# Layers 1 to 3 of a four-layer convolution stack: statistics and quantisation in other steps of a round, layer 1 two chunks behind layer 2, zeros written at the edges only

## The chip, the cores and the metric

The kernel runs on one core of one Trainium2 chip. The metric is the device time of one execution in microseconds (us). Shown are the times of three runs and their median; the profile is of one more execution, whose own time stands beside its span in the table below.

## What is computed

The input x is 32 images of 8 channels of 256 x 256, f32. Four layers follow each other, each of the form x + conv(group norm(x)), with 4 groups of 2 channels:

```python
def _gn(v, G=4, eps=1e-5):           # mean and variance over a group of one image
    ...
x = x + _L0_conv_ref(_gn(x), ...)    # a coupled map lattice of 15 steps, a small network, a gate
x = x + _L1_conv_ref(_gn(x), w, b)   # 3x3, 8 -> 8, on values quantised to +-127
x = x + _L2_conv_ref(_gn(x), w, b)   # 3x3, 8 -> 8, f32
x = x + _L3_conv_ref(_gn(x), w)      # 5x5 mean of each channel
```

Layer 1 quantises with one scale for the whole batch, `sx = 127 / max|gn(x)|`, so it cannot begin before layer 0 has ended for all 32 images. The values of layer 1 are whole numbers up to 127 and are held in bf16; everything else is f32.

## The kernel before

Layer 0 (lines 168 to 676) takes most of the time and isn't touched. Its last step for each image leaves the mean and 1/deviation in `stat1`, the largest normalised value in `peak1`, and the image in DRAM (`x1_d`).

**Layout of layers 1 to 3 (from line 679).** One image is one tile of 128 partitions x 4096: a partition is a pair of (one of 16 rows of a block, one of 8 channels), and the free axis holds 16 blocks of 256 columns. A 3x3 convolution of two blocks (512 columns, one PSUM tile `psv`, one chunk) is `conv3`, line 721: three matmuls over all 128 partitions, one for each column offset (L725), and one for the rows that lie in the neighbouring blocks (L729). The latter reads a small tile of neighbours (`qb` for layer 1, `xb2` for layer 2) of 72 partitions, of which 48 carry data: `beside`, line 138, fills them by two DMAs of 24 partitions from the image's own tile (`qh`, `xh`), issued from the SP queue. An f32 matmul is two records in the profile, a bf16 matmul one. There are 8 chunks (NCH) in an image.

**Tiles and zeros.** `qh`, `qb`, `xh`, `xb2`, `xr` and `xr2` are made once and are reused by all images; lines 718 and 719 set them wholly to zero, on POOL (GpSimd), before the loop. Later only the inner part is rewritten, so that the borders stay zero. The loads of `x1` (L736) are issued from the POOL queue too, behind those memsets. The quantisation scale (`top`, line 150, and lines 694 to 708) is made on DVE in the same stretch.

**A round.** The loop at line 863 runs 35 rounds. In round b, layer 1 works on image b, layer 2 on image b-1, the normalisation of layer 3 on image b-2 and layer 3 itself on image b-3. The order on each engine is the program's order, written out by hand (`manual_schedule`)[...].

The first part of a round is `layer3`, a generator of 8 steps (two for each of 4 groups; PE: L811 and L824, DVE: the addition L831). `among` (line 844) runs one step and then the tasks listed for that step. The tasks in before are

- steps 0 to 3: one piece each of the statistics of layer 2's output (`parts3`) and of layer 1's output (`parts`). `stats_parts`, line 95, has after its first piece, L101, these four: a matmul that averages means (L104) and four small DVE operations (L105 to L108); a second matmul (L111) and one DVE operation (L112); a square root on ACT (L115); five small DVE operations (L117 to L121)
- steps 0 to 3: `quantize1`, a quarter of the image each (DVE L741, L703, L704, then ACT L705), called q0 to q3 below
- step 3: `normal2` (DVE L760, 128 x 4096) ahead of q3, and its two DMAs for `xb2`
- step 4: the two DMAs for `qb`
- step 5: `by_group` (line 127), the statistics of layer 2's output by channel group: two DVE operations (L131), a matmul (L133) that waits for them, and a copy (L135)

The second part of a round runs layers 2 and 1 by turns: one chunk of layer 2 (PE L725, L729; DVE L770 adds, L771 gathers statistics), then one chunk of layer 1 (PE the same lines with bf16; ACT L754, DVE L755 and L756), eight times. In its first four turns `normal3` (DVE L792) prepares layer 3's input `xr`, and after the fourth `beside3` issues two DMAs. At the end of the round `begin` adds up both statistics (L101), the 16 stores of layer 2's output go out from the POOL queue (L776), and the load of `y` for layer 3 (L785) and of the next `x1` stand behind them.

Of the kernel before, what the change touches and what calls it, by code (L numbers as in the profile page):

```python
# [9 lines left out]
F32 = mybir.dt.float32  # L10
BF16 = mybir.dt.bfloat16
# [9 lines left out]
HB = 16  # L21
RB = H // HB
HP, WP = H + 2, W + 2
# [37 lines left out]
def window(ap, offset, dims):  # L61

    return bass.AP(ap.tensor, ap.offset + offset, [list(d) for d in dims])
# [3 lines left out]
def kernel(  # L67
# [3 lines left out]
    nc = tc.nc  # L71
    B = x.shape[0]
# [54 lines left out]
    def by_group(psum, st):  # L127

        sel = small.tile([P, 4, 2], F32, name="sel")
        for j in range(2):  # L130
            nc.vector.tensor_scalar(sel[:, :, j], gsel_sb, st[:, j : j + 1], None, ALU.mult)  # L131
        ps = psum.tile([P, 512], F32, name="ps")
        nc.tensor.matmul(ps[:, 0:8], ones, sel.rearrange("p a b -> p (a b)"), start=True, stop=True)  # L133
        got = small.tile([P, 4, 2], F32, name="got")
        nc.vector.tensor_copy(got.rearrange("p a b -> p (a b)"), ps[:, 0:8])  # L135
        return got

    def beside(queue, t, src, q):


        row, long = HB * WP, (HB - 1) * WP - 2
        for i, (p, to, at) in enumerate(((P - C, 1, 0), (0, 0, 1))):
            queue.dma_start(
                t[q + 24 * i : q + 24 * i + 24, :, :].rearrange("p k w -> p (k w)")[
                    :, to * WP : to * WP + long
                ],
                window(src, p * row + at * WP, [[row, C], [1, 3], [1, long]]),
            )
# [19 lines left out]
    with ExitStack() as es:  # L168
        wt = es.enter_context(tc.tile_pool(name="wt0", bufs=1))
# [5 lines left out]
        psum = es.enter_context(tc.tile_pool(name="ps_a", bufs=3, space=PSUM))  # L175
# [503 lines left out]
    with ExitStack() as es:  # L679
        wt = es.enter_context(tc.tile_pool(name="wt1", bufs=1))  # L680
        two = es.enter_context(tc.tile_pool(name="two", bufs=2))
        psum = es.enter_context(tc.tile_pool(name="ps_b", bufs=3, space=PSUM))
# [19 lines left out]
        def quantize(dst, t, s):  # L702
            nc.vector.tensor_scalar(t, t, s, MAX_Q, ALU.mult, ALU.min)  # L703
            nc.vector.tensor_scalar(t, t, -MAX_Q, ROUND, ALU.max, ALU.add)  # L704
            nc.scalar.activation(dst, t, AF.Copy, bias=-ROUND)  # L705
# [3 lines left out]


        qh = wt.tile([P, HB, WP], BF16, name="qh")
        qb = wt.tile([72, HB, WP], BF16, name="qb")
        xh = wt.tile([P, HB, WP], F32, name="xh")
        xb2 = wt.tile([72, HB, WP], F32, name="xb2")

        xr = wt.tile([P, 2, C, W + 4], F32, name="xr")
        xr2 = wt.tile([72, C, W + 4], F32, name="xr2")
        for t in (qh, qb, xh, xb2, xr, xr2):
            nc.gpsimd.memset(t, 0.0)

        def conv3(src, near, w, i):
            ps = ps_v.tile([P, 512], F32, name="psv")
            o = ps.rearrange("p (k w) -> p k w", w=W)
            for dx in range(3):
                nc.tensor.matmul(  # L725
                    o, w[:, dx, :], src[:, 2 * i : 2 * i + 2, dx : dx + W],
                    start=dx == 0, stop=False,
                )
            nc.tensor.matmul(  # L729
                o, w[0:72, 3, :], near[:, 2 * i : 2 * i + 2, 0:W], start=False, stop=True  # L730
            )
            return ps

        def load1(b):
            x1 = two.tile([P, NPX], F32, name="x1")
            nc.gpsimd.dma_start(x1, x1_d[b])  # L736
            return x1

        def quantize1(b, x1, k):
            t = two.tile([P, 1024], F32, name="tq")  # L740
            nc.vector.tensor_scalar(  # L741
                t, x1[:, bass.ts(k, 1024)], stat1[:, b, 0:1], stat1[:, b, 1:2],
                ALU.subtract, ALU.mult,
            )
            quantize(
                qh[:, 4 * k : 4 * k + 4, 1 : 1 + W],
                t.rearrange("p (r w) -> p r w", w=W), sc[:, 0:1],
            )
# [10 lines left out]
        def normal2(x2, st):  # L759
            nc.vector.tensor_scalar(  # L760
                xh[:, :, 1 : 1 + W], x2.rearrange("p (k w) -> p k w", w=W),
                st[:, 0:1], st[:, 1:2], ALU.subtract, ALU.mult,
            )
            beside(nc.sync, xb2, xh, 0)

        def layer2(b, x2, bn):
            for i in range(NCH):
                ps = conv3(xh, xb2, w2_sb, i)
                c = x2[:, bass.ts(i, 512)]
                nc.vector.scalar_tensor_tensor(c, ps, b2_sb, c, ALU.add, ALU.add)  # L770
                nc.vector.bn_stats(bn[:, i, :], c)  # L771
                yield
            x3 = x3_d[b % 2]
            for r in range(RB):
                m = r % 4 * 4 + r // 4
                nc.gpsimd.dma_start(  # L776
                    window(x3, r * W, [[H * W, C], [RB * W, HB], [1, W]]),
                    x2[C * m : C * m + C, :].rearrange("p (k w) -> p k w", w=W),
                )
# [10 lines left out]
        def normal3(y, gs, g):  # L790
            for k in range(2):
                nc.vector.tensor_scalar(  # L792
                    xr[:, k, 2 * g : 2 * g + 2, 2 : 2 + W], y[:, k, 2 * g : 2 * g + 2, :],
                    gs[:, g, 0:1], gs[:, g, 1:2], ALU.subtract, ALU.mult,
                )
# [46 lines left out]
        x1s, x2s, ys, gss, sums = {}, {}, {}, {}, {}  # L842

        def among(work, tasks):
            for i in range(8):
                next(work, None)
                for task in tasks.get(i, ()):
                    task()
            for _ in work:
                pass  # L850

        def step(parts):
            return lambda: next(parts, None)

        def begin(bn):
            st = small.tile([P, 2], F32, name="st")
            parts = stats_parts(psum, bn, st, gavr_sb, "ps")
            next(parts)
            return st, parts

        with tc.manual_schedule():
            x1s[0] = load1(0)
            for b in range(B + 3):
                if b + 1 < B:
                    x1s[b + 1] = load1(b + 1)
                tasks = {i: [] for i in range(8)}
                if 2 <= b <= B + 1:
                    st3, parts3 = sums.pop(2)
                    for i in range(4):
                        tasks[i].append(step(parts3))  # L870

                    def groups():
                        gss[b - 2] = by_group(psum, st3)

                    tasks[5].append(groups)
                if 1 <= b <= B:
                    st, parts = sums.pop(1)
                    for i in range(4):
                        tasks[i].append(step(parts))
                    tasks[3].append(lambda: normal2(x2s[b - 1], st))  # L880
                if b < B:
                    for k in range(4):
                        tasks[k].append(lambda k=k: quantize1(b, x1s[b], k))
                    tasks[4].append(lambda: beside(nc.sync, qb, qh, 0))
                among(layer3(b - 3, ys.pop(b - 3)) if b >= 3 else iter(()), tasks)
                tasks = {}
                if 2 <= b <= B + 1:
                    for g in range(4):
                        tasks[g] = [lambda g=g: normal3(ys[b - 2], gss[b - 2], g)]
                    tasks[3].append(beside3)  # L890
                bns = [small.tile([P, NCH, 6], F32, name="bn") for _ in range(2)]
                if b < B:
                    x2s[b] = two.tile([P, NPX], F32, name="x2")
                ones_ = layer1(b, x1s[b], x2s[b], bns[0]) if b < B else iter(())

                def both():
                    for _ in layer2(b - 1, x2s[b - 1], bns[1]) if 1 <= b <= B else range(8):
                        next(ones_, None)
                        yield

                among(both(), tasks)
                if 1 <= b <= B:
                    sums[2] = begin(bns[1])
                    ys[b - 1] = load3(b - 1)
                if b < B:
                    sums[1] = begin(bns[0])
# [136 lines left out]
```

## Time and profile before

| | us |
|---|---|
| three runs | 16305.33, 16277.27, 16303.53 |
| median | 16303.53 |
| the profiled execution, its time | 16318.33 |
| its span | 16316.6 |
| mean granted clock of PE | 0.961 |

Busy time over the span, of the page: PE 15452.2 (95%), DVE 11705.9 (72%), ACT 5726.7 (35%), POOL 5598.2 (34%). The page's slices of the span are 407.9 us each; the 34th, where PE falls to seven tenths and POOL to three, is the passage from layer 0 to the rest. The last operation of layer 0 on DVE (L581) is at 13611.19, and layers 1 to 3 take from there to the end, some 2,700 us.

| line, operation | count | mean ns |
|---|---|---|
| L725 PE, layer 2, 128x512 f32 | 1536 | 629 |
| L725 PE, layer 1, 128x512 bf16 | 768 | 384 |
| L729 PE, layer 2, 72 rows, f32 | 512 | 600 |
| L729 PE, layer 1, 72 rows, bf16 | 256 | 399 |
| L811 PE, layer 3 | 2560 | 600 |
| L824 PE, layer 3, 72 rows to 32 columns | 512 | 608 |
| L760 DVE normal2 | 32 | 2415 |
| L741, L703, L704 DVE, a quarter of the quantisation | 128 each | 834, 791, 719 |

How to read it: a matmul's duration in the records is longer than the distance to the next one, since matmuls overlap; PE's pace is read from start to start. A wait is shown as idle time before an instruction with the instruction or DMA that ended it. PE's clock is halved in stretches, and the page gives the granted share in tenths.

### The profile page before, as it was taken

How to read it: one execution, taken by the hardware profiler on the slowest of the kernel's cores; microseconds unless marked ns; L12 is line 12 of the kernel's file. 1: busy time of each engine (PE TensorE's matmuls, PEld its weight loads, DVE VectorE, ACT ScalarE, POOL GpSimd, SP SyncE). 2: the span in 40 equal slices, each digit the busy share in tenths (PEclk: the TensorE clock that was granted, in tenths of full speed). 3: DMA queues.
4: the chain of work that ended last, by engine and by line, in shares of the span. 5: the costliest groups of instructions: out<-in, count | busy, mean ns of one | idle time of the engine just before them, and what ended most of it. 6: DMA issues, size and time to landing. Idle time of an engine off the chain costs nothing.

```text
span 16316.6 us, 141125 instructions
## 1 busy us (share of the span) xinstructions
PE 15452.2 (95%) x42888; PEld 6215.7 (38%) x42888; DVE 11705.9 (72%) x14652; ACT 5726.7 (35%) x8862; POOL 5598.2 (34%) x9491
## 2 busy tenths in 40 slices
PE   6999999999999999999999999999999997999999
PEld 2333333333333333333333333333333332333333
DVE  7777777777777777777777777777777764555554
ACT  2433444443434434443434444343444442111110
POOL 1333333333333333333333333333333342111111
PEclk7999999999999999999999999999999998999999
DMA  4766666666666666666666666666666664555554
GB/s 104 148 146 144 150 147 144 147 150 146 149 144 148 150 147 147 144 147 145 147 142 149 148 144 147 141 148 146 147 149 147 146 134 98 119 119 119 119 118 105
DMA packets 1057742, 2276.12 MB, mean 139 GB/s; under 512 B 419740, under 2 KB 623508, under 8 KB 1050724
## 3 DMA queue, kind: packets, MB, share of 16 engines
q0 software_dynamic: 704512, 1492.80, 40.6%
q1 hardware_dynamic: 352484, 774.29, 23.4%
q8 instruction: 356, 5.83, 0.2%
q14 instruction: 390, 3.19, 0.1%
HBM read 1078.04 MB, written 471.38 MB: 95 GB/s over the span
## 4 chain that ended last, share of the span: by engine, by line
PE 74%; DVE 13%; DMA 7%; ACT 3%; issue 2%; SPq 1%; POOL 0%; DVEq 0%; ACTq 0%; POOLq 0%
PE ph L633 17%; PE psc L391 14%; PE psc L393 13%; PE pg L531 9%; DVE acc L338 7%; PE psv L725 5%; PE pn L610 5%; PE psv L811 4%; DMA qb<-qh 3%; DMA rings<-state 2%; PE psv L729 2%; PE pq L548 1%; PE pg L543 1%; PE pg L539 1%; DVE psc L402 1%
## 5 line engine op out<-in xcount | busy, mean ns | idle before, releaser
L338 DVE SCALAR_TENSOR_TENSOR acc<-strip,taps_sb,acc 128x1024 f32<-128x1024 f32 x3840 | 4930.4, 1284 | 124.8 <-DMA strip<-strip 4.7
L505 POOL DMA_DIRECT2D im<-xn_d x6144 | 3458.3, 566 | 3250.0 <-PE ph L633 1434.7
L633 PE MATMUL ph<-im,wp_sb 72*128 72x512 f32 x8192 | 4091.7, 615 | 308.8 <-ACT hh L638 251.3
L638 ACT ACTIVATE hh<-ph,bp_sb 128x512 f32<-128x512 f32 x4096 | 2755.8, 690 | 4441.9 <-PE ph L633 4385.7
L402 DVE SCALAR_TENSOR_TENSOR psc<-psc,flat 128x512 f32<-128x512 f32 x2880 | 1921.4, 696 | 2813.0 <-PE psc L393 2797.2
L391 PE MATMUL psc<-state,patch_sb 128*128 128x512 f32 x5760 | 2812.0, 626 | 74.1 <-ACT state L419 63.3
L393 PE MATMUL psc<-rings,ring_sb 80*128 80x512 f32 x5760 | 2713.5, 607 | 129.8 <-DMA rings<-state 129.8
L633 PEld LDWEIGHTS ph<-im,wp_sb 72*128 72x128 f32 x8192 | 1489.5, 193 | 2425.4 <-issue 1587.8
L419 ACT ACTIVATE state<-psc,minus 128x512 f32<-128x512 f32 x2688 | 1690.2, 690 | 1818.8 <-DVE psc L402 1713.1
L391 PEld LDWEIGHTS psc<-state,patch_sb 128*128 128x128 f32 x5760 | 1114.5, 199 | 1696.2 <-issue 1375.7
L393 PEld LDWEIGHTS psc<-rings,ring_sb 80*128 80x128 f32 x5760 | 1114.7, 194 | 1576.8 <-issue 1545.7
L569 POOL DMA_DIRECT2D x_d<-xc x256 | 146.9, 574 | 3493.1 <-DVE xc L564 3416.6
L811 PE MATMUL psv<-xr,w_sb 128*128 128x512 f32 x2560 | 1162.9, 600 | 1.3 <-DVE xr L792 1.3
L610 PE MATMUL pn<-hh,wu_sb 128*32 128x512 f32 x8192 | 1133.9, 609 | 3.3 <-ACT hh L638 3.3
L776 POOL DMA_DIRECT2D x_d<-x x512 | 321.0, 643 | 1941.0 <-DVE x L770 1696.3
L725 PE MATMUL psv<-xh,w_sb 128*128 128x512 f32 x1536 | 753.0, 629 | 9.6 <-issue 9.6
L531 PE MATMUL pg<-xq,wg_sb 128*128 128x512 f32 x1536 | 749.3, 626 | 0.0
L754 ACT ACTIVATE x<-psv,b_sb,sc 128x512 f32<-128x512 f32 x256 | 199.3, 779 | 1466.2 <-PE psv L729 1465.8
L531 PE MATMUL pg<-cq,wg_sb 128*128 128x512 f32 x1536 | 713.7, 601 | 0.0
L811 PEld LDWEIGHTS psv<-xr,w_sb 128*128 128x128 f32 x2560 | 466.1, 189 | 610.8 <-issue 606.0
L338 DVE SCALAR_TENSOR_TENSOR acc<-strip,taps_sb,d 128x1024 f32<-128x1024 f32 x480 | 613.2, 1277 | 0.0
L831 DVE TENSOR_TENSOR y<-psv,y 128x512 f32<-128x512 f32 x256 | 177.1, 692 | 593.7 <-PE psv L811 593.7
(163 smaller groups left out, 12188.9 us busy)
## 6 DMA issues: line engine op xcount, KB each, us to landing
im<-xn_d POOLq DMA_DIRECT2D x6144, 96.6 KB, 6.6
rings<-state SPq DMA_DIRECT2D x1920, 159.5 KB
rings<-state SPq DMA_DIRECT2D x1920, 106.3 KB
strip<-strip SPq DMA_DIRECT2D x960, 126.0 KB
xn_d<-xb POOLq DMA_DIRECT2D x128, 516.0 KB, 7.7
nr_d<-xb POOLq DMA_DIRECT2D x128, 516.0 KB, 7.2
xq<-nr_d POOLq DMA_DIRECT2D x128, 516.0 KB, 5.1
cq<-cr_d POOLq DMA_DIRECT2D x128, 516.0 KB, 7.9
```

What stands on the lines that cost most here:

```text
L338: nc.vector.scalar_tensor_tensor(acc, strip[:, dy : dy + RQ, dx : dx + W], taps_sb[:, 3 * dy + dx : 3 * dy + dx + 1], d2 if dy == 1 and dx ...
L391: nc.tensor.matmul(pss[-1], patch_sb[:, c, :], inner(c), start=True, stop=False)
L393: nc.tensor.matmul(pss[c % HALF], ring_sb[:, c, :], rings[half][:, c % HALF, 0 : TX * SY].rearrange("p (x y) -> p x y", y=SY)[:, :, 0:TY], ...
L402: nc.vector.scalar_tensor_tensor(ps, ps, FLOOR, dr[:, c], ALU.max, ALU.add)
L419: nc.scalar.activation(inner(c), pss[c % HALF], AF.Square, bias=minus)
L505: nc.gpsimd.dma_start(im[24 * dy : 24 * dy + 24, k, 0:run], window(xn_d[b % 3], at, [[HP * WP, C], [1, 3], [1, run]]),)
L531: nc.tensor.matmul(o, wg1_sb[:, s, dx, :], src[:, :, dx : dx + W], start=s == dx == 0, stop=False,)
L610: nc.tensor.matmul(pn[32 * q : 32 * q + 32, :], wu_sb[:, i, :], hh, start=i == 0, stop=i == 3,)
L633: nc.tensor.matmul(ph.rearrange("p (k w) -> p k w", w=W), wp_sb, im[:, :, j * WP : j * WP + W], start=True, stop=True,)
L638: nc.scalar.activation(hh, ph, AF.Relu, bias=bp_sb)
L725: nc.tensor.matmul(o, w[:, dx, :], src[:, 2 * i : 2 * i + 2, dx : dx + W], start=dx == 0, stop=False,)
L811: nc.tensor.matmul(pss[k].rearrange("p (c w) -> p c w", w=W), w3_sb[:, dx, :], xr[:, k, mine, dx : dx + W], start=dx == 0, stop=stop,)
```

## The change

Layer 0 isn't touched (its lines move by one). In layers 1 to 3:

- **Zeros.** Only borders are set to zero, by twelve small memsets on DVE; `xr2` alone keeps its memset on POOL. `qb` and `xb2` shrink to the 48 partitions that carry data, and the edge matmul (L740 in the new file) reads 48 rows.
- **Statistics of layer 1's output**: the four pieces stand in steps 0, 0, 1, 1 (they stood in 0 to 3), and `normal2` with its DMAs in step 1 (it stood in step 3).
- **Statistics of layer 2's output**: in steps 1 to 4 (they stood in 0 to 3). `by_group` is split: its DVE part in step 4, its matmul and copy in step 6 (both stood in step 5).
- **Quantisation**: q0 in step 0, q1 and q2 in step 2, q3 in step 3 (they stood in 0, 1, 2, 3), and the DMAs for `qb` in step 3 (they stood in step 4).
- **Layer 1 runs two chunks behind layer 2**: turns 0 and 1 have layer 2 alone, turns 2 to 7 both, and the last two chunks of layer 1 follow one after the other.

```diff
     def by_group(psum, st):
         ...
+        yield None
         ps = psum.tile([P, 512], F32, name="ps")
         ...
-        return got
+        yield got
...
-        qb = wt.tile([72, HB, WP], BF16, name="qb")
+        qb = wt.tile([48, HB, WP], BF16, name="qb")
         xh = wt.tile([P, HB, WP], F32, name="xh")
-        xb2 = wt.tile([72, HB, WP], F32, name="xb2")
+        xb2 = wt.tile([48, HB, WP], F32, name="xb2")
...
-        for t in (qh, qb, xh, xb2, xr, xr2):
-            nc.gpsimd.memset(t, 0.0)
+        for t in (qh, xh):
+            for w in (0, WP - 1):
+                nc.vector.memset(t[:, :, w : w + 1], 0.0)
+        for t in (qb, xb2):
+            for k in (0, HB - 1):
+                nc.vector.memset(t[:, k, :], 0.0)
+        for k in range(2):
+            for w in (0, W + 2):
+                nc.vector.memset(xr[:, k, :, w : w + 2], 0.0)
+        nc.gpsimd.memset(xr2, 0.0)
...
-                o, w[0:72, 3, :], near[:, 2 * i : 2 * i + 2, 0:W], start=False, stop=True
+                o, w[0:48, 3, :], near[:, 2 * i : 2 * i + 2, 0:W], start=False, stop=True
...
+                if 1 <= b <= B:
+                    st, parts = sums.pop(1)
+                    for i in range(4):
+                        tasks[i // 2].append(step(parts))
+                    tasks[1].append(lambda: normal2(x2s[b - 1], st))
                 if 2 <= b <= B + 1:
                     st3, parts3 = sums.pop(2)
                     for i in range(4):
-                        tasks[i].append(step(parts3))
+                        tasks[i + 1].append(step(parts3))
+                    parts4 = by_group(psum, st3)
+                    tasks[4].append(step(parts4))
 
                     def groups():
-                        gss[b - 2] = by_group(psum, st3)
-
-                    tasks[5].append(groups)
-                if 1 <= b <= B:
-                    st, parts = sums.pop(1)
-                    for i in range(4):
-                        tasks[i].append(step(parts))
-                    tasks[3].append(lambda: normal2(x2s[b - 1], st))
+                        gss[b - 2] = next(parts4)
+
+                    tasks[6].append(groups)
                 if b < B:
                     for k in range(4):
-                        tasks[k].append(lambda k=k: quantize1(b, x1s[b], k))
-                    tasks[4].append(lambda: beside(nc.sync, qb, qh, 0))
+                        tasks[(0, 2, 2, 3)[k]].append(lambda k=k: quantize1(b, x1s[b], k))
+                    tasks[3].append(lambda: beside(nc.sync, qb, qh, 0))
...
                 def both():
-                    for _ in layer2(b - 1, x2s[b - 1], bns[1]) if 1 <= b <= B else range(8):
-                        next(ones_, None)
+                    twos = layer2(b - 1, x2s[b - 1], bns[1]) if 1 <= b <= B else iter(range(8))
+                    for i, _ in enumerate(twos):
+                        if i > 1:
+                            next(ones_, None)
                         yield
+                    for _ in ones_:
+                        pass
```

## The prediction

> **What bounds the kernel now.** The changed lines run only after the last stage-0 matmul, so I first read the slices of the page (PE at nine tenths nearly everywhere, a dip at the 34th) and then, for 13,590 us to the end, PE's timeline, PE's waits and DVE's timeline. In the steady rounds PE is never more than a few microseconds from its next matmul, so a round costs PE's own work plus its waits. PE's waits from 13,900 to 16,150 us (total, times, longest):
>
> ```profile
> PE psv L729 <- DMA qb<-qh: 104.9, 28, 5.6
> PE ps L133 <- DVE sel L131: 28.4, 27, 1.1
> ```
>
> Two waits per round are all there is. PE's timeline of one round shows both and what follows (start, length, instruction, idle before it):
>
> ```profile
> 14291.24 8.85 PE L811 MATMUL psv<-xr,w_sb 128*128 128x512 f32 x20
> 14300.02 1.05 PE L824 MATMUL psv<-xr,w3h_sb 72*32 72x512 f32 x4
> 14301.01 1.98 PE L811 MATMUL psv<-xr,w_sb 128*128 128x512 f32 x4
> 14304.04 0.39 PE L133 MATMUL ps<-sel,ones 128*128 128x8 f32 x2 [1.05 <-DVE sel L131]
> ...
> 14399.22 0.81 PE L725 MATMUL psv<-qh,w_bf 128*128 128x512 bf16 x3
> 14403.53 0.39 PE L729 MATMUL psv<-qb,w_bf 72*128 72x512 bf16 x1 [3.50 <-DMA qb<-qh]
> 14403.76 4.44 PE L725 MATMUL psv<-xh,w_sb 128*128 128x512 f32 x6
> ...
> 14409.77 0.59 PE L725 MATMUL psv<-xh,w_sb 128*128 128x512 f32 x1
> ```
>
> The reader is to see that after the 3.50 us wait six L725 records take 4.44 us, where undisturbed they take 2.74 us: the wait is paid once more in a slower clock. Rounds 3 to 31 are 81.57 us apart (L133 starts at 13815.58 in round 3 and at 16099.44 in round 31: 2283.86 / 28). A round that kept its clock, 15201.15 to 15279.75, took 78.60, with a qb wait of 2.47 (2.63 from the start due to the start seen) and 1.21 at L133 (the four L811 records ahead take 1.82, so it could have started at 14302.83 above). Pure PE work is then 78.60 - 2.63 - 1.21 = 74.76 us, and 6.81 us of a mean round is lost.
>
> The entry to these layers, on DVE and POOL:
>
> ```profile
> 13597.84 13.32 DVE L580 TENSOR_SCALAR ext<-ext,stat 128x2 f32<-128x2 f32 x1
> 13605.78 5.36 POOL L719 MEMSET xr<- 128x4160 f32 x2
> 13611.06 1.07 POOL L736 DMA_DIRECT2D x<-x_d  x2
> 13619.34 0.81 DVE L741 TENSOR_SCALAR tq<-x,stat 128x1024 f32<-128x1024 f32 x1 [3.07 <-DMA x<-x_d]
> ```
>
> A 128x2 operation takes 13.32 us and ends 0.02 us after POOL's last memset; the first load of x1 stands behind those memsets too.
>
> [...] The trace shows only the 128x32 mode of L824: 20 L811 records to L824 take 8.78 us against 20 x 0.429 = 8.58, L824 to L811 takes 0.99 against 0.86. A visit to another mode thus costs about 0.20 + 0.13 = 0.32 us. [...]
>
> **The change, part by part.**
>
> *Entry.* Five of six POOL memsets go (17.8 of 19.6 us); twelve small DVE ones come (L88 and L211 take 0.17 and 0.06, so some 1.5 us, partly inside waits of that chain). L580 falls from 13.32 to some 0.2. It then ends near 13599.3; the chain from 13611.19 to L704's end took 5.1, so the first quantising could start at 13604.6. The x1 load waits for the last x_d store (issued after DVE's 13591.85 and the remaining memset, landing in 2.4), starts at 13596.2 and lands in 8.2: 13604.4. So about 13605 against 13619.34: **14 us gained**. In round 1 normal2 stands behind one quantise (2.24 us) instead of three, less a wait for ACT: DMA xb leaves 2.1 us earlier, in round 2 2.6 us, and both times layer 2 waits for xb. Together **18.7 us**.
>
> *qb's wait.* q3 moves from behind two statistics and normal2 to right behind the second L831 of step 3, and layer 1 starts two chunks later. From the start of layer 3 (14354.28) the qb DMA left after 29.3 us (14383.57) and landed 20.0 later; now it leaves at 14375.6 + 2.25 + 1.06, plus 2.3 of new waits, 27.0 after; lands at 47. Layer 1's first edge matmul comes three layer-2 chunks into the second part, at about 55. Eight us of room; the wait (3.75 mean, plus 0.16 of uncovered issue) and the half clock (81.57 - 74.76 - 3.91 - 1.21 = 1.69) go. **5.6 gained per round.** The SP queue has no new entries; xb's DMA moves 10 us earlier on it, clear of qb's.
>
> *L133.* sel is made two steps before its matmul, DVE free there: **1.21 gained**.
>
> *New waits of PE.* In step 0 L104 and L111 stand directly one after the other. From L104's start (14357.72) DVE's L105 starts 0.31 later, L108 ends at 14358.77, L111 could start 0.06 after that; PE would have gone on 0.11 after L104: **1.0 lost**, with layer 3 queued behind it. In step 1 layer 2's L105 stands behind normal2 on DVE. L831 ends at 14365.38, five small operations, normal2 from 14366.27, L105 at 14368.59 (2.32 from start to start), L108 ends at 14369.33. PE, with L104 and eight L811 records from 14364.49, is at L111 at 14368.07: **1.3 lost** (0.9 to 2.1[...]; the largest lengthening of a quantise in the trace is 0.4). The mv of layer 1 comes later, since chunks 6 and 7 run back to back at 0.87 on PE and 1.34 on DVE: 0.5 lost if PE takes 0.87, nothing if it is slower.
>
> *The 48-row edge matmuls.* Their stream of 512 columns is the same. But the built program gives them tile 64x128, where those of 72 rows had 128x128; every chunk of layers 1 and 2 now goes to another mode and back. No row of the trace has this. From below: nothing (a gain is excluded, the matmuls stay in order and as long). [...] Over 8 + 8 chunks, 32 switches: 16 by 0.20 and 16 by 0.14, **5.4 lost per round**. It takes away the 0.5 above.
>
> *Sum against the profiled run, 16318.33 (span 16316.6).* Round: 74.76 + 1.0 + 1.32 + 5.44 = 82.52 against 81.57, + 0.95 over 29 rounds = + 28. Entry - 18.7; rounds 1 and 2 pay the switches, + 11; round 0 hides them behind DVE. Round 32 (no quantising, no qb wait): 3.2 + 1.0 + 1.3 - 1.2 = + 4.3. Round 33 saves L133: - 1.2. Sum: 28 - 18.7 + 11 + 4.3 - 1.2, about + 24. The profiled run lies 14.8 above the median of the runs, so 16303.5 + 24 = **16328**. What is late next is PE itself; y, loaded by about 48 us after layer 3's start, is wanted by normal3 near 48, but five psv tiles give PE ten more.
>
> **Rivals.**
> *A: switches cost as estimated.* 16328, own range 16270 to 16390 (switches 3.5 to 7.5 a round, the second new wait 0.9 to 2.1).
> *B, faster[...].* [...] For: no row of this trace has a row mode, and 72-row matmuls cost nothing extra. Round 74.76 + 0.5 + 1.0 + 1.3 = 77.6, - 4.0 x 29 = - 116, entry - 18.7, rounds 32 and 33 + 0.4: 16169.
> *C, slower: the two new waits put the clock down.* Place: L111 in steps 0 and 2. Price: 1.7 each, what one half-clock spell costs now: 29 x 3.4 = 99, 16427. It decides once a wait with its bubbles comes near 2.5 us, since 2.47 sometimes did it and 1.05 never; against it, I make the waits 1.0 and 1.3.
> *D: the qb wait stays,* because its DMA is held on the queues: + 5.6 x 29, near 16490. For it: the DMA takes 20 us for 181 KB; against: 8 us of room and the longest wait 5.6.
>
> **How the numbers follow.** A 0.62, B 0.27, C 0.08, D 0.03. About 0.2% (33 us) is what a measurement here can tell. A is faster by more than that in 0.13 of its cases, slower in 0.44. Faster: nearly all of B and 0.08 of A: 0.35. Slower: 0.27 of A and C and D: 0.38. Same 0.27. The range leaves out the lower part of B and of the upper end C and D: 16160 to 16395.
>
> **What would show it.** Entry: L580's row under 1 us, the first tq operation 14 us earlier. PE's waits: qb gone, L133 gone, L111 waiting for t twice a round at 1.0 and 1.3. Switches: distance from L725's last record to the edge matmul, 0.63 instead of 0.43 in f32. Wrong would make it: 0.43 there (then B), half-clock stretches after L111 (C), or a qb wait still in the list (D).

## The result, and the profile after

| | us |
|---|---|
| before, median of 13 runs (lowest, highest) | 16291.28 (16265.42, 16309.70) |
| after, median of 13 runs (lowest, highest) | 16328.24 (16311.73, 16370.88) |
| ratio after to before, 95% interval | 1.0024 (1.0015 to 1.0032) |
| the profiled execution after, its time and span | 16323.95, 16322.2 |
| mean granted clock of PE in it | 0.966 (before 0.961) |

The changed kernel is slower by 0.24% (37 us by the medians). The two profiled executions differ by 5.6 us of span only: in layer 0, which the change doesn't touch, the one of after happened to be 25.5 us shorter (its last L564 starts at 13564.97; the same operation, L563, at 13590.43 before). So I compare from there on, where the profiled execution of after is 31.1 us longer. Lines of the new file are one higher in layer 0; further on L725 is now L736, L729 is L740, L811 is L822, L133 is L134, and layer 1's eviction on ACT is L765.

PE's waits from 13,900 to 16,150 us (total, times, longest):

```profile
PE ps L111 <- DVE t L108: 51.6, 54, 1.3
PE psv L736 <- ACT x L765: 23.4, 27, 0.9
```

Both waits that led this list before are gone, the one for qb and the one for sel (the operand of L133). One of the new ones, twice a round at L111, was in the sum. The other, once a round for ScalarE, was not: there PE waits until ScalarE has emptied a PSUM bank (L765, an eviction). PE's timeline of one round (start, length, instruction, idle before it):

```profile
14334.56 0.28 PE L104 MATMUL ps<-mv,gavr_sb 128*128 128x1 f32 x2
14335.67 0.38 PE L111 MATMUL ps<-t,gavr_sb 128*128 128x1 f32 x2 [0.83 <-DVE t L108]
...
14347.30 0.38 PE L111 MATMUL ps<-t,gavr_sb 128*128 128x1 f32 x2 [1.14 <-DVE t L108]
...
14380.21 1.12 PE L740 MATMUL psv<-xb,w_sb 48*128 48x512 f32 x2
14381.26 2.84 PE L736 MATMUL psv<-xh,w_sb 128*128 128x512 f32 x6
...
14394.89 0.82 PE L736 MATMUL psv<-qh,w_bf 128*128 128x512 bf16 x3
14395.64 0.39 PE L740 MATMUL psv<-qb,w_bf 48*128 48x512 bf16 x1
14396.90 2.84 PE L736 MATMUL psv<-xh,w_sb 128*128 128x512 f32 x6 [0.87 <-ACT x L765]
```

The reader is to see three things. L111 starts 1.11 us after L104 in step 0. From edge matmul to next matmul is 1.05 us for two f32 records here (14380.21 to 14381.26); with 72 rows it was 0.86 (14398.36 to 14399.22 in the profile before). And six f32 records of layer 2 stand 0.87 us idle behind an eviction by ScalarE.

DVE's timeline at the entry:

```profile
13572.22 0.29 DVE L581 TENSOR_SCALAR ext<-ext,stat 128x2 f32<-128x2 f32 x1
13580.82 0.81 DVE L752 TENSOR_SCALAR tq<-x,stat 128x1024 f32<-128x1024 f32 x1 [3.21 <-DMA x<-x_d]
```

and POOL's:

```profile
13565.85 1.83 POOL L730 MEMSET xr<- 72x2080 f32 x1 [6.92 <-DVE gt L564]
13572.57 1.07 POOL L747 DMA_DIRECT2D x<-x_d  x2 [4.40 <-DVE ext L581]
```

L581 takes 0.29 us where it took 13.32. One memset is left, and the load of x1 goes out when L581 has ended; DVE then waits for that load alone.

Where the time went, from the last L564 (L563 before) on. A round is counted here from layer 3's first matmul (L822, L811 before), since the groups' matmul (L134, L133 before) has itself moved by a step:

| stretch | before | after | difference |
|---|---|---|---|
| last L564 to the first quantisation | 28.90 | 15.85 | -13.05 |
| from there to round 3 | 164.83 | 170.01 | + 5.2 |
| rounds 3 to 31 (29 rounds) | 2365.68 | 2402.16 | + 36.5 |
| round 32 | 69.00 | 73.11 | + 4.1 |
| rounds 33 and 34, to the end | 97.72 | 96.05 | - 1.7 |

A round has two parts. From layer 3's first matmul to layer 2's first took 41.50 us before and takes 42.61 now; layers 1 and 2 took 40.27, with half-clock stretches in most rounds (PE's granted clock 0.50, 3.4 or 6.8 us at a time), and take 40.03, nearly without them (medians, 13,900 to 15,900 us).

### The profile page after: what moved, and what is told of

It reads as the page before. It is cut to its first block, busy times and chain, and to the rows that moved or that the text cites. A ratio compares the mean times of both kernels' runs of the same rounds, so it can differ in the third digit from the quotient of the medians.

```text
span 16322.2 us, 141095 instructions
## 1 busy us (share of the span) xinstructions
PE 15551.4 (95%) x42888; PEld 6136.8 (38%) x42888; DVE 11681.0 (72%) x14664; ACT 5720.5 (35%) x8862; POOL 5601.3 (34%) x9486
## 5 line engine op out<-in xcount | busy, mean ns | idle before, releaser
L822 PE MATMUL psv<-xr,w_sb 128*128 128x512 f32 x2560 | 1172.1, 602 | 1.3 <-DVE xr L803 1.3
L787 POOL DMA_DIRECT2D x_d<-x x512 | 365.0, 728 | 1709.9 <-DVE x L781 1478.5
L736 PE MATMUL psv<-xh,w_sb 128*128 128x512 f32 x1536 | 738.2, 617 | 33.2 <-ACT x L765 26.0
L765 ACT ACTIVATE x<-psv,b_sb,sc 128x512 f32<-128x512 f32 x256 | 199.0, 777 | 1561.9 <-PE psv L740 1561.9
L822 PEld LDWEIGHTS psv<-xr,w_sb 128*128 128x128 f32 x2560 | 461.7, 189 | 598.0 <-issue 583.4
L414 DVE SCALAR_TENSOR_TENSOR strip<-acc 128x1024 f32<-128x1024 f32 x448 | 549.9, 1227 | 15.3
```

The source lines that it names most:

```text
L736: nc.tensor.matmul(o, w[:, dx, :], src[:, 2 * i : 2 * i + 2, dx : dx + W], start=dx == 0, stop=False,)
L822: nc.tensor.matmul(pss[k].rearrange("p (c w) -> p c w", w=W), w3_sb[:, dx, :], xr[:, k, mine, dx : dx + W], start=dx == 0, stop=stop,)
```

## Experiments

**Theory.** The order of the tasks brings what it should (no wait for qb, none for sel), and three things take it away again: tile switches of the 48-row matmuls, the two waits at L111, and a wait for a PSUM bank. **Rivals.** The new order itself costs the time and the rows nothing; or the waits are such that, if one is removed, the next reader is late in its place.

All runs in one table. The parts are medians; the round is the mean of rounds 3 to 31, from L134's start to the next (L133's before); a half-clock stretch lengthens a mean and not always a median. "Alone" means that everything else is as before. Before was timed anew beside each group of runs (medians of 16290 to 16337 us), and each ratio is to the one beside it.

| version | layers 1, 2 | layer 3 | round | ratio to before (95%) |
|---|---|---|---|---|
| before | 40.27 | 41.50 | 81.57 | 1 |
| after | 40.03 | 42.61 | 82.84 | 1.0024 (1.0015 to 1.0032) |
| e1: after, 72 rows | 35.59 | 43.06 | 78.65 | 0.9933 (0.9920 to 0.9945) |
| e2: 48 rows alone | 44.16 | 41.61 | 85.83 | 1.0094 (1.0080 to 1.0108) |
| e7: after, 72 rows in layer 1 | 38.14 | 43.07 | 81.21 | 0.9989 (0.9982 to 0.9995) |
| e3: e1, statistics spread | 35.59 | 40.74 | 76.33 | 0.9888 (0.9872 to 0.9904) |
| e4: after, six banks | 40.03 | 42.62 | 82.90 | 1.0019 (1.0013 to 1.0026) |
| e5: e3, own banks for layer 1 | 34.45 | 40.80 | 75.27 | 0.9879 (0.9863 to 0.9895) |
| e6: lag of two chunks alone | 35.59 | 41.83 | 77.67 | 0.9922 (0.9908 to 0.9935) |
| e11: e5, lag of one | 34.45 | 40.35 | 74.94 | 0.9869 (0.9855 to 0.9884) |
| e12: e5, no lag | 34.45 | 40.19 | 74.64 | 0.9850 (0.9833 to 0.9867) |
| e13: e1, no lag | 34.45 | 42.51 | 76.97 | 0.9896 (0.9878 to 0.9914) |
| e8: zeros at the edges alone | 39.95 | 41.50 | 81.17 | 0.9995 (0.9986 to 1.0004) |
| e10: before with what helped | 35.06 | 40.58 | 75.93 | 0.9890 (0.9873 to 0.9906) |

### e1: the changed kernel with 72 rows

```diff
-        qb = wt.tile([48, HB, WP], BF16, name="qb")
+        qb = wt.tile([72, HB, WP], BF16, name="qb")
-        xb2 = wt.tile([48, HB, WP], F32, name="xb2")
+        xb2 = wt.tile([72, HB, WP], F32, name="xb2")
...
-                o, w[0:48, 3, :], near[:, 2 * i : 2 * i + 2, 0:W], start=False, stop=True
+                o, w[0:72, 3, :], near[:, 2 * i : 2 * i + 2, 0:W], start=False, stop=True
...
             x1s[0] = load1(0)
+            nc.vector.memset(qb, 0.0)
...
+                if b == 0:
+                    tasks[3].append(lambda: nc.vector.memset(xb2, 0.0))
```

> The changed kernel with its edge matmuls over 72 rows again (qb, xb2 and the weights of the fourth tap group have 72 partitions; the two tiles are zeroed whole by VectorE in layer 1's entry); the order of the tasks, the lag of two chunks and the zeros at the edges of the other tiles stay. Theory (the 48-row matmuls run in a 64x128 tile and each change of tile costs some 0.1 us): all edge matmuls are 128x128 again, each start-to-start spacing around them falls from about 0.52 to 0.43 us (f32) and from 0.31 to 0.22 us (bf16), a full round goes from 82.64 to about 77.9 us, the kernel to about 16328 - 4.75 x 29 - 2 x 4.75 = 16180, or up to 14 us more if half a microsecond of the wait for mv's multiply that the switches covered comes back: 16180 to 16195, 0.6 to 0.7% under the kernel before. Rival (the new order of the tasks and its waits cost the time, not the rows): rounds stay at 82.6 us and the kernel at about 16328.

Measured: 16209.76 where before, timed beside it, had 16312.06: 0.67% less. PE's timeline, where the same chunks as above stand close again:

```profile
14350.44 1.02 PE L737 MATMUL psv<-xb,w_sb 72*128 72x512 f32 x2
14351.30 2.74 PE L733 MATMUL psv<-xh,w_sb 128*128 128x512 f32 x6
```

Its waits on PE, 13,900 to 16,000 us:

```profile
PE ps L111 <- DVE t L108: 51.3, 54, 1.1
PE psv L733 <- ACT x L762: 22.6, 26, 0.9
PE ps L104 <- DVE mv L101: 7.7, 27, 0.3
```

The part of layers 1 and 2 falls by 4.44 us, the part of layer 3 grows by 0.45: the third line, L104 waiting for mv (the means and variances that L101 makes), is that 0.45 (0.88 us from the last matmul to L104 in place of 0.43, in one of the two a round). The undisturbed round falls from 82.64 to 78.65, 3.99 less. The profiles show what changes at an edge: before, with 72 rows too, the load of the edge's weights starts with the matmul ahead of the edge, 0.43 us before the edge itself (14397.93 and 14398.36); in after it starts only together with the edge (both at 14380.21). The rows are the greater part of what the change loses, and the rival that they cost nothing is out.

### e2: 48 rows alone in the kernel before

```diff
-                o, w[0:72, 3, :], near[:, 2 * i : 2 * i + 2, 0:W], start=False, stop=True
+                o, w[0:48, 3, :], near[0:48, 2 * i : 2 * i + 2, 0:W], start=False, stop=True
```

> The kernel before with one part of the change alone: its edge matmuls read 48 rows of both operands instead of 72 (order, tiles and memsets stay as they were). Theory (tile switches): spacings around the edge matmuls grow by 0.09 to 0.10 us each, 32 switches a round, 4.75 us a round, 29 full rounds and about 2 for the ends: 16291 + 147 = about 16440, 0.9% slower than the kernel before; less by up to 2 us a round if the longer matmuls fill part of the wait for qb (16380). Rival (fewer rows are free or cheaper): 16291 or a little less.

Measured: 16475.51 against 16312.06, 163 us more, and the ratio says 0.80 to 1.08% slower. The round is 4.26 us longer. PE's waits, 13,900 to 16,000 us:

```profile
PE psv L729 <- DMA qb<-qh: 80.3, 24, 4.5
PE ps L133 <- DVE sel L131: 26.3, 25, 1.1
```

The wait for qb is a little shorter than before (3.3 us each against 3.7); slower matmuls ahead of it would fill a part of it. The loss by the cut rows is not a consequence of the new order: it is as large without it.

### e7: only layer 1's edge matmul over 72 rows

```diff
-        qb = wt.tile([48, HB, WP], BF16, name="qb")
+        qb = wt.tile([72, HB, WP], BF16, name="qb")
...
-        def conv3(src, near, w, i):
+        def conv3(src, near, w, i, n=48):
...
-                o, w[0:48, 3, :], near[:, 2 * i : 2 * i + 2, 0:W], start=False, stop=True
+                o, w[0:n, 3, :], near[:, 2 * i : 2 * i + 2, 0:W], start=False, stop=True
...
-                ps = conv3(qh, qb, w1_bf, i)
+                ps = conv3(qh, qb, w1_bf, i, 72)
```

> The changed kernel with layer 1's edge matmul alone over 72 rows (qb of 72 partitions); layer 2's stays at 48. Theory (each entry to and exit from a 48-row matmul costs by itself): the spacings at layer 1's edge go back to 0.22 us, 0.19 us for each of the eight chunks, 1.5 us a round, and layer 2's stay at 0.52 to 0.53: 29 x 1.5 + 1.5 = 45 us under the changed kernel, about 0.1% under the kernel before (ratio 0.9995). Rival 1 (the layers share the loss by their number of switches, 16 of 32): half of what the undo of both brought, 70 us under the changed kernel. Rival 2 (only the f32 matmuls pay): the same time as the changed kernel.

Measured: 16287.11, ratio 0.9989, where after had 1.0024: about 57 us below after (0.0035 of 16310), uncertain by some 17, the two intervals put together. PE's timeline:

```profile
14401.75 2.84 PE L735 MATMUL psv<-xh,w_sb 128*128 128x512 f32 x6
14404.52 1.12 PE L739 MATMUL psv<-xb,w_sb 48*128 48x512 f32 x2
14405.58 0.82 PE L735 MATMUL psv<-qh,w_bf 128*128 128x512 bf16 x3
14406.24 0.38 PE L739 MATMUL psv<-qb,w_bf 72*128 72x512 bf16 x1
14406.46 2.74 PE L735 MATMUL psv<-xh,w_sb 128*128 128x512 f32 x6
```

From layer 1's three matmuls to the next f32 one takes 0.88 us (14405.58 to 14406.46), and 1.07 with 48 rows (14385.09 to 14386.16 in after). And the six f32 records behind a 72-row edge take 2.74, those behind a 48-row edge 2.84. The part of layers 1 and 2 falls by 1.89 of the 4.44; the other 2.55 belong to layer 2's edge. The expected 1.5 counted two distances a chunk and left out those 0.10 in the records that follow. By the time alone the run can't choose between 45 us and rival 1's 70; the trace can: layer 1 and layer 2 do not pay alike, and both pay.

### e3: statistics spread over the steps

```diff
-                if 1 <= b <= B:
-                    st, parts = sums.pop(1)
-                    for i in range(4):
-                        tasks[i // 2].append(step(parts))
-                    tasks[1].append(lambda: normal2(x2s[b - 1], st))
...
+                for i in range(3):
+                    if 1 <= b <= B:
+                        tasks[min(i, 1)].append(step(parts))
+                    if 2 <= b <= B + 1:
+                        tasks[min(i, 1)].append(step(parts3))
+                if 1 <= b <= B:
+                    tasks[2].append(step(parts))
+                    tasks[2].append(lambda: normal2(x2s[b - 1], st))
...
+                if 2 <= b <= B + 1:
+                    tasks[3].append(step(parts3))
```

> The 72-row version of the changed kernel with the pieces of the statistics spread out: both layers' first piece in step 0, both second and third pieces in step 1, layer 1's last piece with normal2 and q1, q2 in step 2, q3 with qb's transfer and layer 2's last piece in step 3, the selection in step 4, the groups in step 6. Theory: L104's and L111's matmul are no longer neighbours and layer 2's L111 does not stand behind normal2 on VectorE, so the waits of 0.97 and 1.24 us a round go: 30 rounds x 2.2 = 66 us below the 72-row version without this, about 16120 to 16130. Rival (those waits only move, since some other reader of VectorE is late instead, qb's transfer above all): no more than 10 us from the 72-row version.

Measured: 16136.67, 73 us below e1; the part of layer 3 falls by 2.32, the rest stays. PE's waits, 13,900 to 16,000 us:

```profile
PE psv L733 <- ACT x L762: 24.3, 28, 0.9
PE ps L104 <- DVE mv L101: 7.7, 27, 0.3
```

L111 is out of the list and nothing took its place. The two waits were 2.2 us of the round, and what made them is the place of the matmul: behind its own first half, and behind `normal2`.

### e4: six banks for the convolutions

```diff
-        psum = es.enter_context(tc.tile_pool(name="ps_b", bufs=3, space=PSUM))
-        ps_v = es.enter_context(tc.tile_pool(name="ps_v", bufs=5, space=PSUM))
+        psum = es.enter_context(tc.tile_pool(name="ps_b", bufs=2, space=PSUM))
+        ps_v = es.enter_context(tc.tile_pool(name="ps_v", bufs=6, space=PSUM))
```

> The changed kernel with one PSUM bank moved from the statistics' pool to the convolutions' (2 and 6 instead of 3 and 5); nothing else. Theory (the wait of layer 2's sixth chunk for ScalarE's eviction of layer 1's chunk directly ahead is a shortage of convolution banks, 0.94 us a round): the wait goes, a round 81.7 us, the kernel 16328 - 27 = about 16301. Rival (the allocator hands out the bank just freed, whatever their number, or the wait moves to the statistics' banks): the wait stays or another takes its place, 16320 to 16340.

Measured: ratio 1.0019, not to be told from after's 1.0024, the parts the same to 0.01 us, and the wait still there, one chunk later in the part. PE's timeline, and after it ACT's:

```profile
14412.27 0.39 PE L740 MATMUL psv<-qb,w_bf 48*128 48x512 bf16 x1
14413.52 2.84 PE L736 MATMUL psv<-xh,w_sb 128*128 128x512 f32 x6 [0.87 <-ACT x L765]
```

```profile
14412.69 0.78 ACT L765 ACTIVATE x<-psv,b_sb,sc 128x512 f32<-128x512 f32 x1 [4.12 <-PE psv L740]
```

Layer 2's chunk starts 0.05 us after the eviction of the chunk directly ahead of it. My theory, a shortage of banks, fell. In the built program of after, layer 2's sixth chunk is given the bank that layer 1's chunk just before it used, while the bank of layer 2's second chunk, which L781 had emptied at 14382.12, goes to a later one. Which bank each chunk gets was settled when the program was built. In e4 the sixth bank shifts the pattern by a chunk: there it is layer 2's seventh that gets the bank of layer 1's chunk just before it.

### e5: banks of its own for layer 1

```diff
-        def conv3(src, near, w, i):
-            ps = ps_v.tile([P, 512], F32, name="psv")
+        def conv3(src, near, w, i, pool=ps_v, name="psv"):
+            ps = pool.tile([P, 512], F32, name=name)
...
-                ps = conv3(qh, qb, w1_bf, i)
+                ps = conv3(qh, qb, w1_bf, i, psum, "ps")
```

> The version with 72 rows and spread statistics, and layer 1's chunks take their PSUM banks from the statistics' pool (three banks, idle in the second part of a round) instead of sharing five with layer 2. Theory (the wait of layer 2's sixth chunk for ScalarE comes from the order in which the shared banks were given out when the program was built: the chunk gets the bank that layer 1's chunk just before it used, though a bank that VectorE had emptied 14 us before lies free): with banks of its own layer 2 never waits for ScalarE, the 0.9 us a round goes, the round falls from 76.33 to about 75.4 us, the kernel to 16137 - 27 = 16110. Rival (the eviction itself is the limit: some bank is always waited for at this place): a wait of 0.5 us or more for ScalarE or VectorE stays in the round's second part, 76.0 us or more a round.

Measured: 16107.58 against 16310.02 for before; the part of layers 1 and 2 falls from 35.59 to 34.45, 1.14 us, and the round from 76.33 to 75.27. PE's waits, 13,900 to 15,900 us, are one line now:

```profile
PE ps L104 <- DVE mv L101: 10.2, 27, 0.4
```

With no more banks in all than before, the wait is gone. The two layers have eight of them between them here, though, where they shared five. e13 below has five shared ones and no such wait, so it is the order in which the shared banks are given out, and not their number.

### e6: the lag alone

```diff
-                    for _ in layer2(b - 1, x2s[b - 1], bns[1]) if 1 <= b <= B else range(8):
-                        next(ones_, None)
+                    twos = layer2(b - 1, x2s[b - 1], bns[1]) if 1 <= b <= B else iter(range(8))
+                    for i, _ in enumerate(twos):
+                        if i > 1:
+                            next(ones_, None)
                         yield
+                    for _ in ones_:
+                        pass
```

> The kernel before with one part of the change alone: layer 1's chunks run two chunks behind layer 2's; 72 rows, the old places of the statistics, of the quantisation and of qb's transfer, and the memsets stay. Theory: qb is needed two of layer 2's chunks later, 2 x 3.44 = 6.9 us, more than the 3.75 us that it was late, so this alone removes the wait for qb and the half clock that follows it, 5.6 us of 81.57 a round, and brings the 0.9 us wait for ScalarE with it: 81.57 - 5.6 + 0.9 = 76.9 us a round, 29 x 4.7 = 136 us under the kernel before, about 16175 where before is 16312 (ratio 0.992). Rival (the wait goes to the next reader, the two-deep chain of VectorE's work and the transfers being as late as before): more than 79 us a round, 16240 or more.

Measured: 16174.24, ratio 0.9922; the round 77.67. PE's waits, 13,900 to 15,900 us:

```profile
PE ps L133 <- DVE sel L131: 27.3, 26, 1.1
PE psv L725 <- ACT x L754: 21.7, 25, 0.9
PE psv L729 <- DMA xb<-xh: 5.1, 5, 1.6
```

The wait for qb and the half clock behind it are gone in all rounds, and the wait for ScalarE is there: the lag brings it, whatever the rest. The round is 0.8 above what I expected; 0.2 of it is L104 waiting for mv (0.65 us from the last matmul to L104 instead of 0.43), 0.2 the five waits for xb, and 0.2 that the wait for the bank costs 1.14 and not 0.9.

### e12 and e13: no lag

e12 is e5, and e13 is e1, with layer 1's chunk right behind layer 2's of the same number:

```diff
-                    for i, _ in enumerate(twos):
-                        if i > 1:
-                            next(ones_, None)
+                    for _ in twos:
+                        next(ones_, None)
```

> The same version with no lag at all: layer 1's chunk follows layer 2's of the same number, as in the kernel before. Theory (qb was 3.75 us late there; its issue comes 2.5 us earlier in the new order): a wait of about 1.3 us a round for qb comes back, the wait for mv goes, 75.27 + 1.3 - 0.5 = 76.0 us a round, about 16130. Rival 1 (the earlier issue suffices by itself, the lag is superfluous): no wait for qb, 74.8 us a round. Rival 2 (qb's landing is set by the traffic beside it and not by its issue, so that it is as late as before): 3 us or more a round, with half clock, 78 us and above.

> The changed kernel with 72 rows and without the lag of two chunks (everything else, the tight places of the statistics and the shared banks too, as the change has it). Theory (with the new places of the quantisation qb comes in time by itself, and what the lag did in this change is to bring the wait for a bank, 1.14 us, and the wait for mv, 0.45 us): neither wait is in the list, none for qb, and of the 78.65 us a round of the 72-row version 77.06 are left, all of it TensorE's own work and the two waits of the statistics, 0.97 and 1.24 us: 29 x 1.6 = 46 us below the 72-row version, ratio to the kernel before 0.9905. Rival (the lag is needed with these places of the statistics, since qb's transfer competes with other work): a wait for qb of 1 us or more, 78 us a round or more.

Measured, e12: 16095.15 against 16336.65, ratio 0.9850, a round of 74.64 us in every one of the 28. PE waits for nothing that the list of waits would show. Its timeline of one round's layer 3:

```profile
14421.60 0.38 PE L737 MATMUL ps<-qb,w_bf 72*128 72x512 bf16 x1
14421.82 3.60 PE L819 MATMUL psv<-xr,w_sb 128*128 128x512 f32 x8
14425.26 0.50 PE L104 MATMUL ps<-mv,gavr_sb 128*128 128x1 f32 x4
14425.62 3.68 PE L819 MATMUL psv<-xr,w_sb 128*128 128x512 f32 x8
...
14432.03 0.50 PE L111 MATMUL ps<-t,gavr_sb 128*128 128x1 f32 x4
```

Of the three expectations rival 1 held: without the lag qb comes in time. My 1.3 us set the second of qb's two transfers here (14.7 us ahead of the second part) against the first one before (12.2). Like with like, the first moves from 12.2 us ahead to 15.4 and the second from between 8.6 and 11.1 to 14.7 (13.5 in one round). Whether its earlier issue or its greater distance from xb's transfer (9.8 us between the two pairs in place of 3.8) brings qb in in time, these runs don't separate.

Measured, e13: 16130.59 against 16290.26; the round 76.97 where I had 77.06. PE's one wait, 13,900 to 15,900 us:

```profile
PE ps L111 <- DVE t L108: 49.4, 52, 1.2
```

With five shared banks, as in before, there is no wait for a bank either: in this built program no chunk of layer 2 gets the bank of layer 1's chunk directly ahead of it. With 72 rows, the lag of this change did nothing but bring the wait for the bank (34.45 in place of 35.59) and the wait for mv (42.51 in place of 43.06). With 72 rows and no lag, the change would have been 1.0% faster than the kernel before.

### e11: a lag of one chunk

```diff
-                        if i > 1:
+                        if i > 0:
```

> The version with 72 rows, spread statistics and banks of its own for layer 1, but layer 1 one chunk behind layer 2 instead of two. Theory: qb is issued 14.7 us ahead of the second part here (12.2 before), so it is needed 3.4 us earlier than with two chunks and still in time: no wait for it; and layer 1 ends with two chunks in a row instead of three, VectorE is done 0.6 us earlier, and the 0.54 us that L104's matmul waits for mv falls away: 75.27 to about 74.8 us a round, 16107 - 14 = about 16093. Rival (one chunk is too few, qb is late): a wait for qb in the list, with half clock after it at times, 75.5 us a round or more.

Measured: ratio 0.9869, the round 74.94, mostly 74.81. One wait is left in the whole stretch of 13,900 to 15,900 us:

```profile
PE ps L104 <- DVE mv L101: 0.5, 1, 0.5
```

As expected. Its gain over e5 and its loss to e12 are within the intervals of the times; the rounds show the order.

### e8: the zeros alone

```diff
-        for t in (qh, qb, xh, xb2, xr, xr2):
-            nc.gpsimd.memset(t, 0.0)
+        for t in (qh, xh):
+            for w in (0, WP - 1):
+                nc.vector.memset(t[:, :, w : w + 1], 0.0)
+        for k in range(2):
+            for w in (0, W + 2):
+                nc.vector.memset(xr[:, k, :, w : w + 2], 0.0)
+        nc.gpsimd.memset(xr2, 0.0)
...
+            nc.vector.memset(qb, 0.0)
...
+                if b == 0:
+                    tasks[3].append(lambda: nc.vector.memset(xb2, 0.0))
```

> The kernel before with one part of the change alone: zeros only at the edges on VectorE (qh, xh, xr), qb and xb2 zeroed whole on VectorE inside the loop, only xr2 left to GpSimd; rounds as before. Theory: the last of layer 0's samples to the first quantisation takes 16 us instead of 28.9, because the two-column multiply behind GpSimd's memsets takes 0.3 us instead of 13.3, and nothing else changes: 13 us less, ratio 0.999 to 0.9995, seen in the trace rather than in the time. Rival (the memsets were hidden behind the load of x1 that follows): no gain in that stretch beyond 3 us.

Measured: ratio 0.9995, no difference that the times can tell. DVE's timeline at the entry:

```profile
13576.29 0.29 DVE L580 TENSOR_SCALAR ext<-ext,stat 128x2 f32<-128x2 f32 x1
13583.74 0.81 DVE L746 TENSOR_SCALAR tq<-x,stat 128x1024 f32<-128x1024 f32 x1 [5.79 <-DMA x<-x_d]
```

From the last L563 (13567.70) to the first quantisation it is 16.04 us, 12.9 less than before. This part of the change gives by itself what the whole gives there.

### e10: the kernel before with what had helped

The edits of e5, e6 and e8 on the kernel before, and the selection a step ahead of its matmul (step 4, matmul in step 6); the statistics, the quantisation and qb's transfer stay where they were.

> The kernel before with what the runs so far showed to help and nothing else: the lag of two chunks, zeros at the edges, the selection a step ahead of its matmul, and banks of its own for layer 1; 72 rows, and the statistics, the quantisation and qb's transfer where they were. Theory: the lag's run had 77.42 us a round; without the bank's 1.14 and the selection's 1.21 it is 75.1, and some waits for xb2 of up to 1.6 us remain in a few rounds; the entry gains 13: 16310 - 29 x (81.57 - 75.1) - 13 = about 16110. Rival (the places of the old statistics lose something that the other waits hid): 76 us a round or more, 16135 or more.

Measured: 16145.48, ratio 0.9890; the round 75.93, between what the theory and the rival said. PE's waits, 13,900 to 15,900 us:

```profile
PE psv L735 <- DMA xb<-xh: 16.1, 22, 2.4
PE ps L104 <- DVE mv L101: 1.2, 8, 0.2
```

xb is late in most rounds, by 0.7 us on average; `normal2`, which sends it off, stands in step 3 here. In e5, where it stands in step 2, there is no such wait. So the old places do lose something that the wait for qb had hidden, if less than a microsecond.

## Why the prediction came out as it did

The time (16328 us) was hit, but the closeness is in part luck. The sum put + 24 us on the median of three runs, 16303.5; the median of thirteen is 16291.3, and the change costs + 37 by the medians and + 31.1 from the end of layer 0 on. And two terms of the round were wrong by about a microsecond each, one up and one down. The runs account for the round; e12's 74.64 us, without a wait, is the measured form of the 74.76 that stood for PE's pure work.

| term of a round | predicted | measured | by |
|---|---|---|---|
| pure PE work | 74.76 | 74.64 | e12 |
| tile switches | 5.44 | 4.44 | e1 |
| L111 right behind L104 | 1.0 | 0.97 | 1.081 less 0.112, L104 to L111 |
| L111 behind normal2 | 1.3 | 1.24 | 1.67 less 0.43, layer 3's matmul to L111 |
| the wait for a bank | none | 1.14 | e5, e13 |
| L111's second record after a wait | none | 0.21 | 0.132 in place of 0.028 from the first record, twice |
| half clock | none | 0.18 | 3 of 28 rounds, 1.7 each |
| sum | 82.52 | 82.82, and 82.84 seen | |

- **Entry: right.** 14 us predicted, 13.05 seen, 12.9 in e8. The x1 load was to follow the last store of x_d; it followed L581, 8.25 us ahead of DVE's first quantisation. With POOL's memsets beside it DVE's two-column multiply took 13.32 us, without them 0.29, and four of the five memsets that it lasted through began after it had. From the first quantisation to round 3 I had 11 of switches less 4.7, + 6.3; it was + 5.2. At their measured price the switches of two rounds are 8.9, and the wait for a bank adds 1.1 in round 2 (in round 1 there is none): + 5.3.
- **qb's wait: right that it goes, wrong in what was needed for it.** The step read landing at 47 us against a first reader at 55, two chunks of lag included. By its own figures the reader without lag stood at 48. e12 and e13 show that the moved quantisation suffices, and e6 that the lag suffices too: two remedies for one wait, and with 72 rows the second costs 1.14 + 0.55 a round (e1 against e13); with 48 rows the switches hide the 0.55. I counted the lag as a part of the gain and looked on its side only for mv.
- **L133: right.** It is not in the list of after.
- **The two waits at L111: right,** each within 0.1 us, and e3 removes both.
- **mv: right.** Nothing beside the switches, and 0.45 where those are gone (I had 0.5).
- **The 48-row matmuls: that the switches cost time was right, the size was not.** The failed term is 16 switches by 0.20 (f32) and 16 by 0.14 (bf16). Both prices were my estimates; what the trace of before shows is the way to L824 and back, 0.20 and 0.13 in f32. Measured from start to start, the way into the edge matmul costs 0.092 (f32) and 0.096 (bf16) more, the edge's second f32 record 0.102, the way out 0.091 to 0.097, and the second record of an f32 matmul that follows 0.105. The 0.20 that I put at every switch into or out of f32 is therefore paid only where a second f32 record comes next (0.09 to 0.10 and another 0.10): six of layer 2's eight chunks are followed by bf16 and pay 0.09 to 0.10 alone on the way out. What takes the 0.09 at the switch itself, these runs don't show. e7 divides the 4.44 into 1.89 for layer 1 (2.24 predicted) and 2.55 for layer 2 (3.2 predicted).
- **The bank: missed.** The step called "what is late next" said that five psv tiles give PE room. It counted the tiles, and not which eviction each chunk waits for. e4 shows that counting was the wrong question: a sixth bank left the wait as it was.
- **The rivals.** B, by which a switch costs nothing, needed 0.43 in f32 before the edge matmul; it was 0.52, about half way to the 0.63 of A. C needed half clock behind the waits at L111; there was none, and the three stretches in 28 rounds all follow the wait for the bank. D needed qb in the list; the 20 us that it goes by are of two transfers of 181 KB each, not of one.
- **The ends: right.** Round 32 cost + 4.1 (4.3 predicted), and the rest gained 1.7 (1.2 predicted). With the entry right too, what the sum missed lies in the 29 full rounds, + 36.5 against + 28.

What moved the whole is seen by adding up: the change takes away 81.57 - 74.64 = 6.9 us of loss a round and brings 8.2 (82.84 - 74.64) of another kind. Left with 72 rows, spread statistics, own banks and no lag (e12), the same idea gives 1.5% (1.33 to 1.67).

## What to carry to other kernels

Before you cut rows of a matmul, see whether the new shape gets another tile of the array than its neighbours: here, saving a third of the rows saved no time (a bf16 edge matmul lasts 0.39 us with 48 rows and 0.38 with 72, in the profiles after and before) and cost 0.19 to 0.39 us for each visit. Where a wait can be removed in two ways, try each alone; the second may be superfluous and have a price of its own, as the lag had in evictions and in a longer tail on VectorE. And when PE waits for an eviction, look for which bank the program gave it before you add banks.

## What the runs showed of the hardware beyond that

- A switch between the 128x128 tile and the 64x128 tile that the built program gives to 48 rows takes 0.09 to 0.10 us in these traces, the same in f32 and bf16, and another 0.10 where the second record of an f32 matmul follows. Between 128 and 72 rows, which the built program both puts in the 128x128 tile, it is nothing (0.429 and 0.428 us to and from the edge).
- Before, half-clock stretches (granted clock 0.50, 3.4 or 6.8 us long) followed the waits for qb, 3.7 us on average, in 24 of 28 rounds; e12, without waits, had no such stretch in its 28. In after there are three and in e4 four, of 3.4 us each. All seven begin within 0.4 us of the end of the 0.87 us wait for the bank, none at the waits at L111, though of those the second is longer; and in e1, e3, e6 and e7, with 72 rows in all or half of the edges, the wait for the bank never did it. What sets off the seven is not shown.
- One small multiply of 128x2 (L580 before) lasted 13.32 us through a series of memsets on GpSimd, and ended only with the last of them (13611.16, the memset at 13611.14).
